# Attention scores in 32x64 tiles, with the keys summed down to 64 rows before the softmax sums

## The chip, the cores and the metric

The kernel runs on one core of a Trainium2 chip. A core has a matmul engine (TensorE, "PE" in the profile, with its weight loads as "PEld"), a vector engine (VectorE, "DVE"), an activation engine (ScalarE, "ACT"), a general engine (GpSimd, "POOL") and a queue engine (SyncE, "SP") that issues the transfers of this kernel. The metric is the device time of one execution in microseconds. All data is fp32.

## The reference

Two layers are applied to x of shape (8, 256, 64, 64). Layer 0 is an attention with 8 heads of 32 channels, in which the 4096 pixels of an image ask 256 keys that a 4x4 convolution with stride 4 makes. Layer 1 is a linear attention with depthwise convolutions, and takes no part in the change. Layer 0, cut to what matters:

```
xr  = conv(x, w_sr, stride 4); xr = layernorm over channels(xr)
q   = w_q x                            # 4096 tokens a batch
k,v = split(w_kv xr)                   # 256 keys a batch
for each of 8 heads (d = 32):
    sim  = q k^T / sqrt(32)            # 4096 x 256
    attn = softmax(sim over the keys)
    out  = attn v
x   = x + gamma * (w_out out)
```

## The kernel before

The kernel has three passes. The first makes layer 0 and the products w_qkv x of layer 1; the second and third do the rest of layer 1. The change is in the first pass, in the functions `keys_values`, `scores`, `valued`, `joined`, `counted`, `copied` and `normed`.

The first pass walks through 128 turns: 8 batches, 8 strips of 512 tokens (QB), 2 halves c of the channels (4 heads each). In a turn, the softmax is computed without a maximum, transposed: keys on partitions, tokens along the columns. `scores` (L820) is called twice a turn, for kc = 0 and 1, the two halves of 128 keys. For each head h it multiplies 32 rows of k (the head's channels, on partitions 32h to 32h+31, 128 keys as columns) with 32 rows of q and 512 tokens; the four heads stand on four different row groups of the array. ScalarE takes exp of each bank (L830) into a tile e of 128 keys by 512 tokens. `valued` (L843) multiplies v (128 keys by 32 channels of a head) with e (128 by 512) and adds the two kc in PSUM; the four heads stand in four column groups. The denominators come from `joined` (L857): GpSimd adds the e of kc = 0 and of kc = 1 for each head (L861); and from `counted` (L865): a matrix of ones (128 by 32) times this sum gives each token's sum over the keys, on 32 partitions. `copied` (L870) takes the product with v out of PSUM on ScalarE. `normed` (L875) turns the sums by 32x32 blocks on VectorE (L881), takes reciprocals of the sixteen columns that are needed, spreads them with a second transpose and multiplies.

The order within turn n is written out in the loop at L1072: first scores of kc = 0 of turn n, then the products with v and the sums of turn n-1, then scores of kc = 1 of turn n and its additions on GpSimd, then copy and normalization of turn n-1. After these come, as a filling for TensorE, products of w_qkv x (`qkv`, L931, seven products for a pair of parts, spread over the following turns), the queries of the next turn (L806), every second turn the output product `added` (L898) and, for turns 6 to 15 of a batch, the convolution and layernorm of the next batch's keys (`keys_values`, L725, a generator that is advanced step by step). A scheduler places instructions of an engine by these priorities; the first five turns of all have no qkv products to fill with. `differences` (L912) makes inputs of qkv, three on VectorE and one on GpSimd (L919), every fourth turn.

PSUM has eight banks, given out in rotation by `bank` (L641). Two are kept out of the rotation while they are in use: "av" from `valued` to `copied`, and "den" from `counted` to the first transpose in `normed`. `given_back` returns them to the end of the rotation.

Tiles on SBUF rotate by their number of buffers: e has 12 (E_BUFS), ej (the sum over kc) 4. `keys_values` uses one ring "ln" of 3 buffers for xr, sq and wide. v of a batch is kept in `vv`, 128 keys by 2 halves by 256 channels; kk and vv have two buffers each, so that the next batch's are made while the present batch's are read.

An fp32 matmul is two MATMUL rows and two LDWEIGHTS rows in the profile.

Of the kernel before, what the change touches and what calls it, by code (L numbers as in the profile page):

```python
# [27 lines left out]
F32 = mybir.dt.float32  # L28
AF = mybir.ActivationFunctionType
ALU = mybir.AluOpType  # L30
# [25 lines left out]
RS = 16  # L56
NS = HH // RS
BR = QB // WW
PE_TAPS = 6


# [563 lines left out]
def first_pass(ctx: ExitStack, tc: tile.TileContext, a, fine, planes, x2d, kd, vd, ready):  # L625
# [15 lines left out]
    def bank(name, keep=None):  # L641
        i = turns.pop(0)
        if keep:
            kept[keep] = i
        else:
            turns.append(i)
        return psum.tile([P, 512], F32, tag=f"bank{i}", name=name)
# [75 lines left out]
    kks, vvs = {}, {}  # L723

    def keys_values(b):  # L725
        ln = lambda name: keys.tile([P, 2, NK], F32, tag="ln", name=f"{name}_{b}", bufs=3)
        xr = ln("xr")

        ps = bank(f"sr_{b}", "sr").rearrange("p (o k) -> p o k", o=2)
        taps = sorted((phase(dy, dx), dy * R + dx) for dy in range(R) for dx in range(R))  # L730
        for f, tap in taps:
            w = keys.tile([P, 2, C], F32, tag="wsr", name=f"wsr_{b}_{f}", bufs=3)
            nc.sync.dma_start(w, a.w_sr[:, :, tap])
            for ci in range(2):
                for oc in range(2):
                    nc.tensor.matmul(  # L736
                        ps[:, oc],
                        w[:, ci, oc * P : (oc + 1) * P],
                        strips(b, f // 2)[:, ci, f % 2 * NK : (f % 2 + 1) * NK],
                        start=(f == ci == oc == 0),  # L740
                        stop=(f == R * R - 1 and ci == 1),
                        skip_group_check=True,
                    )
            yield
        nc.scalar.copy(xr, ps)
        given_back("sr")
        yield

        mean = bank(f"mean_{b}")[:, :NK]
        for ci in range(2):  # L750
            nc.tensor.matmul(mean, mean_w, xr[:, ci], start=(ci == 0), stop=(ci == 1))
        for ci in range(2):
            nc.vector.tensor_sub(xr[:, ci], xr[:, ci], mean)
        sq = ln("sq")
        nc.vector.tensor_mul(sq, xr, xr)
        yield

        var = bank(f"var_{b}")
        for kc in range(2):
            for ci in range(2):  # L760
                nc.tensor.matmul(
                    var[:, kc : kc + 1],
                    sq[:, ci, kc * P : (kc + 1) * P],
                    mean_w[:, 0:1],
                    start=(ci == 0),
                    stop=(ci == 1),
                )
        rstd = two.tile([P, 2, 2], F32, tag="rstd", name=f"rstd_{b}")
        nc.vector.tensor_scalar_add(rstd[:, 0], var[:, 0:2], LN_EPS)
        nc.gpsimd.tensor_tensor(rstd[:, 1], rstd[:, 0], mhalf, ALU.pow)  # L770
        wide = ln("wide")
        nc.scalar.copy(wide[:, :, :P], rstd[:, 1].unsqueeze(2).to_broadcast([P, 2, P]))
        yield
        rs = bank(f"rs_{b}")[:, :NK]
        for kc in range(2):
            nc.tensor.matmul(rs[:, kc * P : (kc + 1) * P], wide[:, kc, :P], ident, start=True, stop=True)
        for ci in range(2):
            nc.vector.tensor_mul(xr[:, ci], xr[:, ci], rs)
            nc.vector.tensor_scalar(
                xr[:, ci], xr[:, ci], consts["vec"][:, 0, ci : ci + 1], consts["vec"][:, 1, ci : ci + 1], ALU.mult, ALU.add  # L780
            )
        yield
        kk = two.tile([P, 2, NK], F32, tag="kk", name=f"kk_{b}")
        vv = two.tile([P, 2, C], F32, tag="vv", name=f"vv_{b}")
        kks[b], vvs[b] = kk, vv
        for oc in range(2):
            ps = bank(f"k_{b}_{oc}")[:, :NK]
            for ci in range(2):
                nc.tensor.matmul(
                    ps, consts["wkv"][:, ci, oc * P : (oc + 1) * P], xr[:, ci], start=(ci == 0), stop=(ci == 1)  # L790
                )
            nc.scalar.copy(kk[:, oc], ps)
        yield
        for kc in range(2):
            ps = bank(f"v_{b}_{kc}")[:, :C]
            for ci in range(2):
                nc.tensor.matmul(
                    ps, xr[:, ci, kc * P : (kc + 1) * P], consts["wkv"][:, ci, C:], start=(ci == 0), stop=(ci == 1)
                )
            nc.scalar.copy(vv[:, kc], ps)  # L800
        yield


# [15 lines left out]

    def scores(b, s, c, kc, qs):  # L820
        scs = [bank(f"sc_{b}_{s}_{c}_{kc}_{h}") for h in range(4)]
        for h in range(4):
            rows = slice(h * D0, (h + 1) * D0)
            nc.tensor.matmul(  # L824
                scs[h], kks[b][rows, c, kc * P : (kc + 1) * P], qs[rows], start=True, stop=True
            )
        es = []
        for h in range(4):
            e = two.tile([P, QB], F32, tag="e", name=f"e_{b}_{s}_{c}_{kc}_{h}", bufs=E_BUFS)
            nc.scalar.activation(e, scs[h], AF.Exp, scale=D0**-0.5)  # L830
            es.append(e)
        return es
# [9 lines left out]

    def valued(b, s, c, kc, es):  # L843
        if kc == 0:
            sums["av"] = bank(f"av_{b}_{s}_{c}", "av")
        for h in range(4):
            cols = slice(h * D0, (h + 1) * D0)
            nc.tensor.matmul(  # L848
                sums["av"][cols],
                vvs[b][:, kc, c * P + h * D0 : c * P + (h + 1) * D0],  # L850
                es[h],
                start=(kc == 0),
                stop=(kc == 1),
            )


    def joined(b, s, c, es0, es1):  # L857
        both = []
        for h in range(4):
            e = halves.tile([P, QB], F32, tag="ej", name=f"ej_{b}_{s}_{c}_{h}", bufs=4)  # L860
            nc.gpsimd.tensor_tensor(e, es0[h], es1[h], ALU.add)  # L861
            both.append(e)
        return both

    def counted(b, s, c, es):  # L865
        sums["den"] = bank(f"den_{b}_{s}_{c}", "den")
        for h in range(4):
            nc.tensor.matmul(sums["den"][h * D0 : (h + 1) * D0], ones_w, es[h], start=True, stop=True)  # L868

    def copied(b, s, c):  # L870
        att[b, s, c] = rest.tile([P, QB], F32, tag="att", name=f"att_{b}_{s}_{c}", bufs=4)
        nc.scalar.copy(att[b, s, c], sums["av"])
        given_back("av")

    def normed(b, s, c):  # L875
        den = sums["den"]
        i = 2 * ((b * NG + s) * 2 + c)
        turn = rest.tile([P, NB, D0], F32, tag="rden", name=f"rden_{b}_{s}_{c}", bufs=1)
        one = two.tile([P, NB], F32, tag="one", name=f"one_{b}_{s}_{c}")

        tc.keep_in_program_order(nc.vector.transpose(turn.rearrange("p n d -> p (n d)"), den))  # L881
        given_back("den")
        nc.vector.reciprocal(one, turn[:, :, 0])
        r = rest.tile([P, NB, D0], F32, tag="rall", name=f"rall_{b}_{s}_{c}", bufs=1)
        nc.vector.transpose(r, one.unsqueeze(2).to_broadcast([P, NB, D0]))
# [1136 lines left out]
```

## Time and profile before

| | before |
|---|---|
| median of 3 runs | 3618.5 us (3616.45 to 3620.99) |
| the profiled execution | 3620.12 us, span 3618.3 us |
| TensorE granted clock | 0.989 |
| PE busy | 3536.7 us (98%), 24738 rows |
| DVE busy | 2221.5 us (61%) |
| POOL busy | 1525.8 us (42%) |
| ACT busy | 1461.8 us (40%) |
| PE in scores, L824 | 292.9 us, 2048 rows |
| PE in products with v, L848 | 248.3 us, 2048 rows |
| PE in sums, L868 | 137.8 us, 1024 rows |
| POOL in additions, L861 | 679.0 us, 512 rows of 1354 ns |

A row of the groups gives line, engine, operation, output and inputs, shapes and count, then the busy time of the group, the mean length of one and the engine's idle time before them with what ended it. "32*128" after a matmul is the part of the array that it uses, rows by columns. Busy times are unions, so that four matmuls side by side count once. In the timeline a row has start, length, engine and line, and merges like instructions; "PE" rows end where a model puts the end, so that a group's cost is better read from the start of the next group.

### The profile page before, as it was taken

What the parts mean: (1) busy time and instruction counts of PE and PEld (TensorE: products, weight loads), DVE (VectorE), ACT (ScalarE), POOL (GpSimd) and SP (SyncE); (2) the same over time, 40 slices, a digit from 0 to 9 for tenths busy, and PEclk for the clock granted to TensorE, in tenths of its full rate; (3) what the DMA queues carried; (4) which work ended last, traced back from release to release, by engine and by line L of the source; (5) the groups of instructions that cost most, each with busy time, mean ns of one, the idle gap of its engine ahead of it and who ended that gap; (6) DMA issues with size and microseconds to landing.
All of it is one profiled execution on the core that took longest, in us unless ns stands there. A gap on an engine that the chain in (4) does not pass through costs nothing.

```text
span 3618.3 us, 64503 instructions
## 1 busy us (share of the span) xinstructions
PE 3536.7 (98%) x24738; PEld 1937.9 (54%) x24738; DVE 2221.5 (61%) x3371; ACT 1461.8 (40%) x3241; POOL 1525.8 (42%) x1506
## 2 busy tenths in 40 slices
PE   8999999999999999999999999999999999999998
PEld 4443534434435344344334788888888874333333
DVE  1557466565574665655777777777777774444442
ACT  2444344354443443544553444444444423333332
POOL 2434344343343443433443566566656541222222
PEclk9999999999999999999999999999999999999999
DMA  5345445455454454553645999999999977787773
GB/s 176 99 113 147 134 98 158 112 140 136 106 148 130 101 156 107 131 147 98 161 116 134 267 250 263 265 259 255 264 264 255 261 236 212 222 228 229 222 220 95
DMA packets 574780, 643.44 MB, mean 178 GB/s; under 512 B 81408, under 2 KB 450560, under 8 KB 574464
## 3 DMA queue, kind: packets, MB, share of 16 engines
q1 hardware_dynamic: 574464, 639.24, 64.0%
q8 instruction: 197, 3.23, 0.4%
q14 instruction: 119, 0.97, 0.1%
HBM read 389.85 MB, written 249.23 MB: 177 GB/s over the span
## 4 chain that ended last, share of the span: by engine, by line
PE 87%; DMA 6%; DVE 3%; ACT 1%; SPq 1%; issue 1%; POOL 0%; POOLq 0%; DVEq 0%; ACTq 0%
PE qkv L946 16%; PE p L1740 11%; PE cv L1313 8%; PE sc L824 8%; PE av L848 7%; PE o L902 6%; PE q L809 6%; PE sr L736 6%; PE cv L1344 6%; PE sums L1399 6%; PE den L868 3%; DMA raw<-planes 2%; DMA vq<-v 2%; PE rep L1726 2%; PE den L1707 1%
## 5 line engine op out<-in xcount | busy, mean ns | idle before, releaser
L861 POOL TENSOR_TENSOR ej<-e,e 128x512 f32<-128x512 f32 x512 | 679.0, 1354 | 950.5 <-ACT e L830 950.5
L830 ACT ACTIVATE e<-sc 128x512 f32<-128x512 f32 x1024 | 529.3, 608 | 568.6 <-PE sc L824 568.6
L1313 PE MATMUL cv<-w,c 128*128 128x128 f32 x3072 | 388.9, 280 | 12.8 <-DVE stage L959 6.7
L1313 PEld LDWEIGHTS cv<-w,c 128*128 128x128 f32 x3072 | 366.1, 195 | 14.6 <-issue 6.7
L1750 POOL TENSOR_TENSOR y<-z,xs 128x512 f32<-128x512 f32 x128 | 165.5, 1302 | 463.1 <-ACT z L1748 434.2
L824 PE MATMUL sc<-q,kk 32*128 32x512 f32 x2048 | 292.9, 639 | 0.0
L946 PE MATMUL qkv<-differences,combined 128*128 128x512 f32 x576 | 291.3, 597 | 0.4 <-POOL differences L919 0.3
L1399 PE MATMUL sums<-vq,r 128*32 128x288 f32 x4096 | 265.5, 408 | 0.0
L1740 PE MATMUL p<-raw,wp 128*128 128x512 f32 x512 | 248.8, 608 | 9.9 <-ACT z L1748 9.9
L848 PE MATMUL av<-e,vv 128*32 128x512 f32 x2048 | 248.3, 598 | 0.6 <-ACT e L830 0.6
L881 DVE STREAM_TRANSPOSE rden<-den 128x512 f32<-128x512 f32 x128 | 91.5, 715 | 254.6 <-PE den L868 252.4
L1330 ACT ACTIVATE r<-s 128x512 f32<-128x512 f32 x128 | 81.0, 632 | 411.8 <-DVE s L1329 402.6
L736 PE MATMUL sr<-x,wsr 128*128 128x256 f32 x1024 | 234.5, 383 | 9.4 <-DMA wsr<-in_w_sr_dram 9.3
L809 PE MATMUL q<-x,wq 128*128 128x512 f32 x512 | 241.9, 594 | 0.0
L1740 PE MATMUL p<-agg,wp 128*128 128x512 f32 x512 | 241.2, 593 | 0.0
L902 PE MATMUL o<-att,wout 128*128 128x512 f32 x512 | 230.4, 592 | 0.0
L736 PEld LDWEIGHTS sr<-x,wsr 128*128 128x128 f32 x1024 | 195.8, 192 | 63.2 <-issue 34.5
L817 ACT COPY q<-q 128x512 f32<-128x512 f32 x128 | 75.1, 586 | 373.4 <-PE q L809 373.4
L962 DVE TENSOR_TENSOR whole<-part,qkv 128x512 f32<-128x512 f32 x256 | 172.7, 684 | 73.4 <-ACT part L1008 54.0
L1344 PE MATMUL cv<-y,w 128*128 128x128 f32 x1536 | 204.0, 278 | 6.9 <-DVE y L1265 4.1
L1399 PEld LDWEIGHTS sums<-vq,r 128*32 128x32 f32 x4096 | 156.0, 110 | 75.2 <-issue 1.2
L946 PE MATMUL qkv<-x,wqkv 128*128 128x512 f32 x384 | 188.8, 611 | 5.2 <-ACT e L830 5.2
(162 smaller groups left out, 5734.8 us busy)
## 6 DMA issues: line engine op xcount, KB each, us to landing
planes<-stage SPq DMA_DIRECT2D x128, 578.0 KB
d<-planes SPq DMA_DIRECT2D x128, 578.0 KB
vq<-v SPq DMA_DIRECT2D x256, 256.0 KB
raw<-planes SPq DMA_DIRECT2D x64, 578.0 KB
x<-in_xp_dram SPq DMA_DIRECT2D x64, 512.0 KB
wsr<-in_w_sr_dram SPq DMA_DIRECT2D x128, 256.0 KB
x<-x SPq DMA_DIRECT2D x128, 256.0 KB
k<-turned SPq DMA_DIRECT2D x256, 128.0 KB
```

Of the source, the lines that this page charges most:

```text
L736: nc.tensor.matmul(ps[:, oc], w[:, ci, oc * P : (oc + 1) * P], strips(b, f // 2)[:, ci, f % 2 * NK : (f % 2 + 1) * NK], start=(f == ci == ...
L809: nc.tensor.matmul(ps, consts["wq"][:, ci, c * P : (c + 1) * P], strips(b, s)[:, ci], start=(ci == 0), stop=(ci == 1),)
L824: nc.tensor.matmul(scs[h], kks[b][rows, c, kc * P : (kc + 1) * P], qs[rows], start=True, stop=True)
L830: nc.scalar.activation(e, scs[h], AF.Exp, scale=D0**-0.5)
L848: nc.tensor.matmul(sums["av"][cols], vvs[b][:, kc, c * P + h * D0 : c * P + (h + 1) * D0], es[h], start=(kc == 0), stop=(kc == 1),)
L861: nc.gpsimd.tensor_tensor(e, es0[h], es1[h], ALU.add)
L902: nc.tensor.matmul(ps, consts["wout"][:, c, oc * P : (oc + 1) * P], att[c], start=(c == 0), stop=(c == 1))
L946: nc.tensor.matmul(ps, w, x, start=True, stop=True)
L1313: nc.tensor.matmul(ps[:, g * P : (g + 1) * P], c[:, g, cols], w[:, g, n * P : (n + 1) * P], start=(da == 0), stop=(da == 1),)
L1344: nc.tensor.matmul(out, w[:, g], x, start=True, stop=True)
L1399: nc.tensor.matmul(ps[h * D0 : (h + 1) * D0, : 36 * D1].rearrange("p (r n e) -> p r n e", r=3, e=D1), kt[:, par, h, 2 * r + c], vq[:, r : ...
L1740: nc.tensor.matmul(as_block(ps, i // 2), wp[:, i, oc * P : (oc + 1) * P], block(g, i // 2, i % 2, j), start=(i == 0), stop=(i == 3),)
```

## The change

In the score products, each head's matmul of 32 rows by 128 keys, 512 tokens, is replaced by four: for each quarter kq of 64 keys and each half of the tokens one of 32 rows by 64 keys and 256 tokens. The two halves of the tokens go to the two halves of the partitions of the output (rows 0 to 63 and 64 to 127), and the two quarters of keys of a kc to its two halves of columns. So a tile e has the same size as before, but its rows 0 to 63 hold 64 keys for the first 256 tokens, rows 64 to 127 the same 64 keys for the last 256 tokens, and its column halves two quarters of keys.

The products with v are done in 64 rows (keys) by 32 columns (channels), 256 tokens: one for each quarter, head and half of the tokens, four quarters added in PSUM. The two halves of the tokens go to two banks, av0 and av1, 256 columns of each. v is needed on both halves of the partitions for every quarter, so `vv` grows to four quarters, ScalarE copies each v product in two halves, and two transfers per batch copy each half to the other partitions.

`joined` adds the e of both kc as before (ej, now with one buffer), then adds the two column halves (ef, 128 by 256): this sums the keys down to 64 rows for each half of the tokens. `counted` multiplies ones of 64 rows by 32 columns with 256 columns of ef, for each head and half, into the other 256 columns of av0 and av1. There is no bank "den" any more; av0 and av1 are given back after the transposes in `normed`, and `copied` and the first transpose are done in two parts of 256 columns. Ring "ln" shrinks to two buffers and wide gets a tile of its own.

```diff
--- before.py
+++ after.py
@@ -56,6 +56,8 @@
 RS = 16
 NS = HH // RS
 BR = QB // WW
+HALVES = slice(0, P // 2), slice(P // 2, P)
+QH = slice(0, QB // 2), slice(QB // 2, QB)
 PE_TAPS = 6
 
 
@@ -723,7 +725,7 @@
     kks, vvs = {}, {}
 
     def keys_values(b):
-        ln = lambda name: keys.tile([P, 2, NK], F32, tag="ln", name=f"{name}_{b}", bufs=3)
+        ln = lambda name: keys.tile([P, 2, NK], F32, tag="ln", name=f"{name}_{b}", bufs=2)
         xr = ln("xr")
 
         ps = bank(f"sr_{b}", "sr").rearrange("p (o k) -> p o k", o=2)
@@ -768,12 +770,12 @@
         rstd = two.tile([P, 2, 2], F32, tag="rstd", name=f"rstd_{b}")
         nc.vector.tensor_scalar_add(rstd[:, 0], var[:, 0:2], LN_EPS)
         nc.gpsimd.tensor_tensor(rstd[:, 1], rstd[:, 0], mhalf, ALU.pow)
-        wide = ln("wide")
-        nc.scalar.copy(wide[:, :, :P], rstd[:, 1].unsqueeze(2).to_broadcast([P, 2, P]))
+        wide = keys.tile([P, 2, P], F32, tag="wide", name=f"wide_{b}", bufs=1)
+        nc.scalar.copy(wide, rstd[:, 1].unsqueeze(2).to_broadcast([P, 2, P]))
         yield
         rs = bank(f"rs_{b}")[:, :NK]
         for kc in range(2):
-            nc.tensor.matmul(rs[:, kc * P : (kc + 1) * P], wide[:, kc, :P], ident, start=True, stop=True)
+            nc.tensor.matmul(rs[:, kc * P : (kc + 1) * P], wide[:, kc], ident, start=True, stop=True)
         for ci in range(2):
             nc.vector.tensor_mul(xr[:, ci], xr[:, ci], rs)
             nc.vector.tensor_scalar(
@@ -781,7 +783,7 @@
             )
         yield
         kk = two.tile([P, 2, NK], F32, tag="kk", name=f"kk_{b}")
-        vv = two.tile([P, 2, C], F32, tag="vv", name=f"vv_{b}")
+        vv = two.tile([P, 4, C], F32, tag="vv", name=f"vv_{b}")
         kks[b], vvs[b] = kk, vv
         for oc in range(2):
             ps = bank(f"k_{b}_{oc}")[:, :NK]
@@ -797,7 +799,10 @@
                 nc.tensor.matmul(
                     ps, xr[:, ci, kc * P : (kc + 1) * P], consts["wkv"][:, ci, C:], start=(ci == 0), stop=(ci == 1)
                 )
-            nc.scalar.copy(vv[:, kc], ps)
+            for h, rows in enumerate(HALVES):
+                nc.scalar.copy(vv[rows, 2 * kc + h], ps[rows])
+        for h, rows in enumerate(HALVES):
+            nc.sync.dma_start(vv[HALVES[1 - h], h::2], vv[rows, h::2])
         yield
 
 
@@ -819,11 +824,17 @@
 
     def scores(b, s, c, kc, qs):
         scs = [bank(f"sc_{b}_{s}_{c}_{kc}_{h}") for h in range(4)]
-        for h in range(4):
-            rows = slice(h * D0, (h + 1) * D0)
-            nc.tensor.matmul(
-                scs[h], kks[b][rows, c, kc * P : (kc + 1) * P], qs[rows], start=True, stop=True
-            )
+        for kq in range(2 * kc, 2 * kc + 2):
+            for h in range(4):
+                rows = slice(h * D0, (h + 1) * D0)
+                for half in range(2):
+                    nc.tensor.matmul(
+                        scs[h][HALVES[half], QH[kq % 2]],
+                        kks[b][rows, c, kq * P // 2 : (kq + 1) * P // 2],
+                        qs[rows, QH[half]],
+                        start=True,
+                        stop=True,
+                    )
         es = []
         for h in range(4):
             e = two.tile([P, QB], F32, tag="e", name=f"e_{b}_{s}_{c}_{kc}_{h}", bufs=E_BUFS)
@@ -842,44 +853,51 @@
 
     def valued(b, s, c, kc, es):
         if kc == 0:
-            sums["av"] = bank(f"av_{b}_{s}_{c}", "av")
-        for h in range(4):
-            cols = slice(h * D0, (h + 1) * D0)
-            nc.tensor.matmul(
-                sums["av"][cols],
-                vvs[b][:, kc, c * P + h * D0 : c * P + (h + 1) * D0],
-                es[h],
-                start=(kc == 0),
-                stop=(kc == 1),
-            )
+            sums["av"] = [bank(f"av_{b}_{s}_{c}_{half}", f"av{half}") for half in range(2)]
+        for kq in range(2 * kc, 2 * kc + 2):
+            for h in range(4):
+                cols = slice(h * D0, (h + 1) * D0)
+                for half, rows in enumerate(HALVES):
+                    nc.tensor.matmul(
+                        sums["av"][half][cols, : QB // 2],
+                        vvs[b][rows, kq, c * P + h * D0 : c * P + (h + 1) * D0],
+                        es[h][rows, QH[kq % 2]],
+                        start=(kq == 0),
+                        stop=(kq == 3),
+                    )
 
 
     def joined(b, s, c, es0, es1):
         both = []
         for h in range(4):
-            e = halves.tile([P, QB], F32, tag="ej", name=f"ej_{b}_{s}_{c}_{h}", bufs=4)
+            e = halves.tile([P, QB], F32, tag="ej", name=f"ej_{b}_{s}_{c}_{h}", bufs=1)
             nc.gpsimd.tensor_tensor(e, es0[h], es1[h], ALU.add)
-            both.append(e)
+            f = halves.tile([P, QB // 2], F32, tag="ef", name=f"ef_{b}_{s}_{c}_{h}", bufs=4)
+            nc.gpsimd.tensor_tensor(f, e[:, QH[0]], e[:, QH[1]], ALU.add)
+            both.append(f)
         return both
 
     def counted(b, s, c, es):
-        sums["den"] = bank(f"den_{b}_{s}_{c}", "den")
         for h in range(4):
-            nc.tensor.matmul(sums["den"][h * D0 : (h + 1) * D0], ones_w, es[h], start=True, stop=True)
+            for half, rows in enumerate(HALVES):
+                nc.tensor.matmul(
+                    sums["av"][half][h * D0 : (h + 1) * D0, QH[1]], ones_w[rows], es[h][rows], start=True, stop=True
+                )
 
     def copied(b, s, c):
         att[b, s, c] = rest.tile([P, QB], F32, tag="att", name=f"att_{b}_{s}_{c}", bufs=4)
-        nc.scalar.copy(att[b, s, c], sums["av"])
-        given_back("av")
+        for half in range(2):
+            nc.scalar.copy(att[b, s, c][:, QH[half]], sums["av"][half][:, : QB // 2])
 
     def normed(b, s, c):
-        den = sums["den"]
         i = 2 * ((b * NG + s) * 2 + c)
         turn = rest.tile([P, NB, D0], F32, tag="rden", name=f"rden_{b}_{s}_{c}", bufs=1)
         one = two.tile([P, NB], F32, tag="one", name=f"one_{b}_{s}_{c}")
 
-        tc.keep_in_program_order(nc.vector.transpose(turn.rearrange("p n d -> p (n d)"), den))
-        given_back("den")
+        flat = turn.rearrange("p n d -> p (n d)")
+        for half in range(2):
+            tc.keep_in_program_order(nc.vector.transpose(flat[:, QH[half]], sums["av"][half][:, QH[1]]))
+            given_back(f"av{half}")
         nc.vector.reciprocal(one, turn[:, :, 0])
         r = rest.tile([P, NB, D0], F32, tag="rall", name=f"rall_{b}_{s}_{c}", bufs=1)
         nc.vector.transpose(r, one.unsqueeze(2).to_broadcast([P, NB, D0]))
```

## The prediction

> **What bounds the kernel now.** I read the page's slices and its chain first: who is busy, and whose work ends last.
>
> ```profile
> PE   8999999999999999999999999999999999999998
> PE 87%; DMA 6%; DVE 3%; ACT 1%; SPq 1%; issue 1%; POOL 0%; POOLq 0%; DVEq 0%; ACTq 0%
> ```
>
> TensorE is busy in nearly every slice and carries 87% of the chain. The change lies in the first pass, about 60 to 1945 us. There I took two whole turns (one turn: 512 tokens, one half of the channels) from the windows view; its columns are length, PE, PEld, DVE, ACT, POOL.
>
> ```profile
> 803.82:816.60 12.78, 12.78 (x63) 4.64 (x59) 8.48 (x13) 6.17 (x15) 5.41 (x4) 1.00 0.85 290
> 816.60:829.38 12.78, 12.78 (x63) 4.64 (x59) 9.63 (x15) 5.58 (x14) 5.54 (x5) 1.00 0.73 145
> ```
>
> TensorE fills all 12.78 us; the others leave 3 us or more. So a microsecond off TensorE's row is a microsecond off the turn, until another engine's chain becomes as long. The timeline of TensorE prices the three groups touched; differences of starts are used, since the ends are modelled.
>
> ```profile
> 802.75 1.14 PE L824 MATMUL sc<-q,kk 32*128 32x512 f32 x8
> 803.82 1.92 PE L848 MATMUL av<-e,vv 128*32 128x512 f32 x16
> 805.56 1.04 PE L868 MATMUL den<-ej,ones_w 128*32 128x512 f32 x8
> 806.53 1.14 PE L824 MATMUL sc<-q,kk 32*128 32x512 f32 x8
> 807.61 1.12 PE L946 MATMUL qkv<-differences,wqkv 128*128 128x512 f32 x2
> ```
>
> Each fp32 matmul is two rows. Scores take 1.07 us, the v products 1.74, the sums 0.97. The weight loads show how they run:
>
> ```profile
> 804.28 0.13 PEld L848 LDWEIGHTS av<-e,vv 128*32 128x32 f32 x4 [0.30 <-issue]
> 804.71 0.13 PEld L848 LDWEIGHTS av<-e,vv 128*32 128x32 f32 x4 [0.30 <-issue]
> ```
>
> Four tiles start together, then 0.43 us pass: a wave of four side by side, 512 columns long. Last, who feeds the sums:
>
> ```profile
> 807.75 2.06 ACT L830 ACTIVATE e<-sc 128x512 f32<-128x512 f32 x4 [0.91 <-PE sc L824]
> 808.43 5.41 POOL L861 TENSOR_TENSOR ej<-e,e 128x512 f32<-128x512 f32 x4 [5.05 <-ACT e L830]
> ```
>
> GpSimd adds from 808.43 to 813.84; the sums that use this start at 818.34. The slack is 4.5 us. These are the rows for prices:
>
> ```profile
> L861 POOL TENSOR_TENSOR ej<-e,e 128x512 f32<-128x512 f32 x512 | 679.0, 1354 | 950.5 <-ACT e L830 950.5
> L868 PE MATMUL den<-ej,ones_w 128*32 128x512 f32 x1024 | 137.8, 592 | 0.4 <-POOL ej L861 0.4
> L1294 POOL TENSOR_TENSOR red_agg<-red_agg 128x256 f32<-128x256 f32 x64 | 57.7, 901 | 5.0
> L1294 POOL TENSOR_TENSOR red_raw<-red_raw 128x256 f32<-128x256 f32 x64 | 53.6, 837 | 2.7
> L1382 PE MATMUL raw<-vq,kq 128*32 128x32 f32 x4096 | 49.3, 199 | 0.0
> ```
>
> **What the Trainium skill says.** "TensorEngine Tiling (Array Packing)", sections Available Configurations and Key Properties: 32×64 and 64×32 both give eight tiles that work independently, and a change of mode drains the array. The trace agrees as far as it goes: four row tiles (scores) and four column tiles (v products) run side by side, and about 0.1 us is lost at each mode change. Eight tiles of rows and columns at once are in no row. "TensorE: Matmul & The Clock Gate", section Measured speedup vs the span model, gives 10.6 times for sixteen 32-by-32 tiles, so rows and columns combine; the trace can't confirm it. The Tiling page's Instruction Overhead gives about 60 cycles for each matmul. The trace is cheaper: 4096 rows of L1382 in 49.3 us, 12 ns each. Eight rows a wave are 0.1 us, below the 0.215 us that a wave of 256 columns lasts. "GPSIMD Engine Reference", Specifications: GpSimd's SBUF interface is shared with VectorE, and suffers from VectorE operations with two SBUF inputs. The trace agrees: most ej take 1.26 us, those beside the multiplication L887 up to 1.72.
>
> **The change, part by part.** TensorE first, for one turn.
>
> Scores (twice): 4 matmuls become 16, each half as wide and half as long. Waves go from 2 of 0.43 to 4 of 0.215: 0.86 us both. Of the 0.21 us beside the waves, about 0.107 is the first weight load of 128 columns (single rows: the first wave lasts 534 ns, the next 427), and about 0.09 the drain. 64 columns halve the load: -0.05. Eight tiles started 6.7 ns apart (single rows) instead of four add 0.03. Group: 1.05, gain 0.02, twice 0.04.
>
> Products with v: 8 matmuls become 32; 4 waves of 0.43 become 8 of 0.215, unchanged. The sums: 4 matmuls of 128 rows by 512 become 8 of 64 rows by 256, 2 waves of 0.43 become 2 of 0.215: -0.43. The later start of eight tiles costs 0.03, once. Sum: -0.04 - 0.43 + 0.03 = -0.44; I take -0.43.
>
> GpSimd: 4 operations of 128x256 more, with L1294 as the nearest row: same width, also dependent on the operation just before. Undisturbed it takes 0.73 us (median of red_raw), disturbed up to 1.1; its wait leaves a gap of 0.08 in the single rows. Since ej has one buffer now, each ej also waits for the ef before it: 0.08 again. So 1.26 + 0.08 + 0.73 + 0.08 = 2.15 for a head, 8.5 for four, and 0.45 for the meeting with L887: 8.96 instead of 5.4. The extra 3.55 us fit into the slack of 4.5 with 0.95 to spare. In the order of the sums it is a loop: scores start, 1.90 until the first addition (806.53 to 808.43), 8.96, 0.55 for the last head's sum and the drain, next scores: 11.4 us. TensorE's turn becomes 12.35 or more, so it stays the longer. Lower bound of the ef: 0.66 (half of an ej); upper: 1.06, every one disturbed.
>
> At the start the loop does decide. The first five turns have no qkv products and take 7.3 to 11.4 us; that part of the trace runs from 60.97 (first ej) to 104.30 (sixth turn's second scores). After: 60.97 + 8.6 + 0.5 = 70.1, then four loops of 11.4: 115.7. Loss: 11 us, gain included. The last turn, 9.99 us now, pays 1.5 the same way.
>
> TensorE's order is the same otherwise, except that in seven turns a product with v or some sums stand apart from their group: 14 more mode changes at 0.15 (drain and load), 2 us.
>
> ScalarE: att in two copies of 0.37 (row L800) for one of 0.60, +0.14, and once a batch four vv copies for two, +0.75: under its 6 us of idle in a turn. These copies now wait for the sums too, which share the bank: about 806.1, and ScalarE isn't free for them before 806.24. VectorE: the transpose L881 (0.715) in two, about +0.15 from the 0.41 of a 128x256 row (L778); 3 us idle cover it. Both banks come back after these transposes, as den's did; six other banks are used first. Without that cover a late bank would stop scores by those tenths.
>
> SP: two more DMAs of 128 KB a batch, behind a wait for the vv copies. Behind them on SP stand two weight loads at the start and stores later; nobody waits for these within microseconds. At the start v must land before 61.5, the copies end near 57.8: I count 0, at most 3 us once. Later batches have v made turns ahead. Fewer ln buffers and a smaller wide: same operations, 0.
>
> Sum: 123 turns × -0.43 = -53; +11 +1.5 +2. The net is -38 against the profiled execution's 3620.1 (span 3618.3): 3582. The median of the runs is 1.6 lower: 3580.
>
> **The rivals.** (A) GpSimd takes over: if the ef meet VectorE's two-input work (differences L917 to L920, L887) as the disturbed half of L1294 did, 1.06 us each, the chain is 10.3, the loop 12.7 to 12.8 in the 56 shortest turns, more where memsets or L919 fall in. For: margin of 0.95 us only. Against: VectorE's work beside additions in the trace mostly reads PSUM, and those ej took 1.26. It decides from about 0.25 us of ef beyond 0.73; at 1.06 replaying the additions after the profile's ready times gives no gain to 20 us loss, with memsets in the chain 60: 3620 to 3680. This is the case on the other side.
>
> (B) The eight tiles don't run side by side. Should row tiles exclude each other in 64×32, the ten waves double: +2.15 - 0.43 = 1.7 a turn, 220 us, 3840; in scores alone +1.3 a turn, 3785; both 4060. For: no row shows it. Against: both forms run singly, and issue at 12 ns suffices.
>
> (C) The gain is there but small: waves of 256 columns carry a fixed cost of 20 ns more, 18 waves are 0.36 us a turn. 3605 to 3625, no change.
>
> **How the numbers follow.** Main case 0.61 (3565 to 3603), A 0.13, B 0.11, C 0.10 (about half beyond -0.2%), still faster 0.05 (no loss at the start, loads wholly hidden: 3555). A measurement tells 0.2%, 7 us, from no change. Faster: 0.61 + 0.05 + 0.05 = 0.71; same: 0.05 of C and 0.03 of A, 0.08; slower: 0.10 of A and B, 0.21. The range leaves out B and the ends of A and of the fast case: 3556 to 3645. The likeliest case alone has 3565 to 3603.
>
> **What would show it.** The sums' group from 0.97 to about 0.5 us between starts, v products still 1.74, scores 1.05; 38000 PE rows instead of 24738; turns of 12.35 for 12.78; ef near 0.75, its chain near 9 us, and no wait of the sums for it after the fifth turn; about 11 us lost by 116 us. The prediction fails if the v products' group grows (B), or if TensorE idles before the sums in the steady turns (A).

## The result and the profile after

The changed kernel takes 3681.3 us (median of 4 runs, 3667.9 to 3683.2); the kernel before, beside it on the same chip, 3617.5 (3616.2 to 3621.0). The ratio is 1.0167, with an interval of 1.0142 to 1.0192: 1.7% slower, where 1% faster was predicted. The profiled execution is the one of 3681.4 us; its span is 3679.6 us, 61.3 more than before.

First the page of the changed kernel: TensorE's slices, and the groups of the two additions.

```profile
PE   7999999999999999999999899999999999999998
L874 POOL TENSOR_TENSOR ej<-e,e 128x512 f32<-128x512 f32 x512 | 660.3, 1290 | 423.1 <-ACT e L841 394.8
L876 POOL TENSOR_TENSOR ef<-ej 128x256 f32<-128x256 f32 x512 | 410.7, 802 | 38.3
```

The slices look as they did; the loss is spread too thin for tenths. The second addition takes 0.80 us on the mean, near the 0.73 that was assumed. The page's chain can't be used here: it reaches back only to 2018 us, past the first pass. Now the timeline of TensorE in a steady turn; differences of starts are read.

```profile
799.93 1.12 PE L831 MATMUL sc<-q,kk 32*64 32x256 f32 x32
800.97 1.96 PE L861 MATMUL av<-e,vv 64*32 64x256 f32 x64
802.73 0.64 PE L883 MATMUL av<-ef,ones_w 64*32 64x256 f32 x16
803.29 1.12 PE L831 MATMUL sc<-q,kk 32*64 32x256 f32 x32
804.34 1.13 PE L964 MATMUL qkv<-differences,wqkv 128*128 128x512 f32 x2
```

Scores 1.04 to 1.05 us (before 1.07), products with v 1.76 (1.74), sums 0.56 (0.97). On TensorE the change does what was predicted. Two turns in the windows view (length, PE, PEld, DVE, ACT, POOL, then clock, share of the transfers and GB/s): turn 35, which lost, and a steady one:

```profile
588.93:603.69 14.76, 13.24 (x164) 6.21 (x163) 8.29 (x13) 6.35 (x16) 11.74 (x15) 1.00 0.52 161
803.29:815.63 12.34, 12.34 (x170) 6.00 (x162) 10.03 (x14) 5.70 (x17) 9.86 (x9) 1.00 0.84 185
```

The steady turn is 12.34 us for 12.78, the predicted gain of 0.44. But not all turns are steady. A turn is measured here from its first score matmul to that of the next, and n is its number. The 127 differences between the kernels sum to +71.4 us, in six kinds of turn:

| turns | count | before to after, us | at -0.44 each it would be |
|---|---|---|---|
| n = 0 to 5, the start | 6 | +14.1 | (predicted +11) |
| n%4 == 3 | 30 | +50.8 | -13.2 |
| n%16 == 9 | 8 | +17.3 | -3.5 |
| n%16 == 12 | 8 | +5.5 | -3.5 |
| n%4 == 2 | 31 | +3.0 | -13.6 |
| the others | 44 | -19.2 | -19.4 |

The kind that lost most, n%4 == 3, has this in GpSimd's timeline around turns 34 and 35 (turn 34 starts at 575.06):

```profile
576.11 0.74 POOL L876 TENSOR_TENSOR ef<-ej 128x256 f32<-128x256 f32 x1
585.25 0.16 POOL L943 MEMSET stage<- 128x68 f32 x1 [8.41 <-DMA planes<-stage]
585.47 0.22 POOL L944 MEMSET stage<- 128x68 f32 x1
585.58 1.26 POOL L874 TENSOR_TENSOR ej<-e,e 128x512 f32<-128x512 f32 x1
```

A "stage" is a tile in which `qkv` collects planes with a border of zeros before they are stored; `new_stage` sets the border on GpSimd (L943, L944). There is one buffer for each of two kinds, so its memset waits until the transfer that stores the older stage has read it. Here this memset stands ahead of the additions of turn 34, and the queue works in order. In the kernel before, the first addition of turn 34 starts 6.7 us after the turn's first scores, and 6.8 us after in the changed kernel with the memsets out of the way (below); here it starts 10.5 us after: 3.7 us late. The sums that need it stand in the next turn on TensorE:

```profile
591.73 0.92 PE L883 MATMUL av<-ef,ones_w 64*32 64x256 f32 x12
594.16 0.62 PE L883 MATMUL av<-ef,ones_w 64*32 64x256 f32 x4 [1.52 <-POOL ef L876]
594.72 1.12 PE L831 MATMUL sc<-q,kk 32*64 32x256 f32 x32
```

Their last head waits, and everything behind on TensorE waits with it. In the kernel before, the same memset was queued behind the additions of that turn, with the next addition 5 us later (at 565.83), and cost nothing:

```profile
553.11 4.96 POOL L861 TENSOR_TENSOR ej<-e,e 128x512 f32<-128x512 f32 x4 [7.74 <-ACT e L830]
560.28 0.16 POOL L925 MEMSET stage<- 128x68 f32 x1 [1.84 <-DMA planes<-stage]
```

### The profile page after: what moved, and what is told of

Read it like the earlier page. It is cut to its first block, busy times and chain, and to the rows that moved or that the text cites. A ratio compares the mean times of both kernels' runs of the same rounds, so it can differ in the third digit from the quotient of the medians.

```text
span 3679.6 us, 92633 instructions
## 1 busy us (share of the span) xinstructions
PE 3530.2 (96%) x38050; PEld 2120.4 (58%) x38050; DVE 2202.6 (60%) x3499; ACT 1484.5 (40%) x3385; POOL 1909.7 (52%) x2018
## 5 line engine op out<-in xcount | busy, mean ns | idle before, releaser
L874 POOL TENSOR_TENSOR ej<-e,e 128x512 f32<-128x512 f32 x512 | 660.3, 1290 | 423.1 <-ACT e L841 394.8
L876 POOL TENSOR_TENSOR ef<-ej 128x256 f32<-128x256 f32 x512 | 410.7, 802 | 38.3
L899 DVE STREAM_TRANSPOSE rden<-av 128x256 f32<-128x256 f32 x256 | 99.8, 428 | 412.6 <-ACT att L890 412.5
L831 PE MATMUL sc<-q,kk 32*64 32x256 f32 x8192 | 296.2, 395 | 0.0
L738 PE MATMUL sr<-x,wsr 128*128 128x256 f32 x1024 | 238.8, 388 | 20.3 <-DMA wsr<-in_w_sr_dram 20.3
L861 PE MATMUL av<-e,vv 64*32 64x256 f32 x8192 | 255.4, 382 | 0.5 <-ACT e L841 0.5
L831 PEld LDWEIGHTS sc<-q,kk 32*64 32x64 f32 x8192 | 155.4, 133 | 150.6 <-issue 104.4
L861 PEld LDWEIGHTS av<-e,vv 64*32 64x32 f32 x8192 | 148.1, 107 | 98.3 <-issue 39.5
```

Of the source, the lines that this page charges most:

```text
L738: nc.tensor.matmul(ps[:, oc], w[:, ci, oc * P : (oc + 1) * P], strips(b, f // 2)[:, ci, f % 2 * NK : (f % 2 + 1) * NK], start=(f == ci == ...
L831: nc.tensor.matmul(scs[h][HALVES[half], QH[kq % 2]], kks[b][rows, c, kq * P // 2 : (kq + 1) * P // 2], qs[rows, QH[half]], start=True, sto ...
L861: nc.tensor.matmul(sums["av"][half][cols, : QB // 2], vvs[b][rows, kq, c * P + h * D0 : c * P + (h + 1) * D0], es[h][rows, QH[kq % 2]], st ...
L876: nc.gpsimd.tensor_tensor(f, e[:, QH[0]], e[:, QH[1]], ALU.add)
```

## The experiments

All ratios are to the kernel before in the same session. "First pass" is the sum over the 127 turns, in the profiled execution, against before (after: +71.4).

**The tiles without the second addition.** In `joined` and `counted`, with ej in four buffers and whole in five (the diff is cut; `...` stands for what was left out):

```diff
-            f = halves.tile([P, QB // 2], F32, tag="ef", ...)
-            nc.gpsimd.tensor_tensor(f, e[:, QH[0]], e[:, QH[1]], ALU.add)
+        for k in range(2):
+            for h in range(4):
+                for half, rows in enumerate(HALVES):
+                    nc.tensor.matmul(sums["av"][half][h * D0 : (h + 1) * D0, QH[1]], ones_w[rows],
+                        es[h][rows, QH[k]], start=(k == 0), stop=(k == 1))
```

> The new tiles for scores, products with v and sums, without the second addition on GpSimd: the sums add both column halves of ej on TensorE (16 matmuls of 64 rows by 256 columns a turn in place of 8), ej has four buffers again and whole five. Theory (the loss comes from the additions on GpSimd and from what stands around them in its queue): TensorE has four waves of 0.215 us for the sums as before, so the turns stay at 12.7 to 12.8 us and the start loses nothing: 3612 to 3622 us. Rival (the small tiles or the shared bank of products and sums cost the time): 3650 us or more.

Measured: 3639.7 us, ratio 1.0060 (1.0042 to 1.0079); first pass +26.2, of which +21.5 lies in the turns n%16 == 9 and +3.1 in n%4 == 2. Neither side was right: the start and the turns n%4 == 3 lost nothing (+0.1 each), but something else did. TensorE's timeline of this kernel in turn 25:

```profile
418.32 1.92 PE L861 MATMUL av<-e,vv 64*32 64x256 f32 x52
421.83 3.72 PE L738 MATMUL sr<-x,wsr 128*128 128x256 f32 x16 [1.59 <-DMA wsr<-in_w_sr_dram]
425.48 0.43 PE L861 MATMUL av<-e,vv 64*32 64x256 f32 x6
```

Eight matmuls of the next batch's reduction (sr, two rows each) stand in the middle of the products with v, and wait for their weights. In this kernel they were put there without any wait for GpSimd. So this split is not the second addition's doing. Nor is the place of the memset: here too it stands ahead of the additions, as in turn 34, which starts at 553.70:

```profile
564.93 0.16 POOL L946 MEMSET stage<- 128x68 f32 x1 [12.93 <-DMA planes<-stage]
565.25 4.97 POOL L874 TENSOR_TENSOR ej<-e,e 128x512 f32<-128x512 f32 x4
```

The four additions start 11.5 us after the first scores, and the turns n%4 == 3 lose nothing. So the scheduler's new order came with the tiles; the longer chain made it dear. The split was taken out by itself: the two steps of sr at the end of the turns n%16 == 8 go to the next turn.

```diff
-        for _ in range(taps):                           # the second two steps of a turn
+        for _ in range(taps * (at != 8)):
-        for _ in range(taps):                           # the first two
+        for _ in range(taps * (2 if at == 9 else 1)):
```

> As e1_tiles_only (new tiles, no second addition on GpSimd), with the two sr steps of the turns n%16==8 left to the next turn as in e3, so that the sums stand together. Theory (the tiles themselves cost nothing; the whole loss of e1 was the sums split by sr matmuls in seven turns, 22 us): 3618 us, the same as before (3611 to 3624). Rival (the tiles or the shared bank cost something of their own in every turn): 3630 us or more.

Measured: 3619.8 us, ratio 1.0001 (0.9990 to 1.0011); the turns n%16 == 9 at 0.0, the first pass at +5.6. The theory holds: 32x64 and 64x32 tiles, the shared bank and the doubled v cost nothing that the times show. The gain of 0.44 us, and the losses at the start and in the turns n%4 == 3 and n%16 == 12, appear only with the second addition. The turns n%4 == 2 stand at +3.2 here as well; they come back below.

**The memsets behind the additions.** The changed kernel with

```diff
-        nc.gpsimd.memset(st[:, :, 0 if g // 2 else NB], 0.0)
+        tc.keep_in_program_order(nc.gpsimd.memset(st[:, :, 0 if g // 2 else NB], 0.0))
```

and the same for the second memset. `keep_in_program_order` holds an instruction behind the one that its engine was given last.

> The changed kernel with one thing moved: the memsets of a stage stand in GpSimd's queue behind the additions of the turn in which they are made, not ahead of them; all other engines keep their order. Theory (a memset that waits for the transfer of the older stage holds up the additions behind it): the turns n%4==3 fall from about 15.1 to 12.3 us, 23 times 2.8, so 3617 us (3608 to 3632). Rival (eight additions a turn are too long for GpSimd wherever the memsets stand): 3665 us or more.

Measured: 3632.3 us, ratio 1.0036 (1.0023 to 1.0049); first pass +21.9. The turns n%4 == 3 went from +50.8 to +3.1. The waits of TensorE for the second addition in the first pass, of the changed kernel and then of this one (total us, times, longest):

```profile
PE av L883 <- POOL ef L876: 29.9, 26, 1.8
```

```profile
PE av L883 <- POOL ef L876: 4.7, 3, 1.8
```

The three waits that are left belong to the start (turns 4 and 5); from turn 6 to 126 there is none. Nothing but the place of memsets in one queue was changed, and 48 of the 64 us that these turns had missed came back (49 over all turns). The chain of eight additions fits, with 0.35 to 1 us between its end and the sums in the steady turns; the rival that it doesn't is out. The time is at the upper edge of what was expected, since 16 us of the 64 did not come back. They lie in the turns n%16 == 11 alone, and have another cause (the power of rstd, below). The first addition of turn 34 now starts 6.84 us after the turn's first scores:

```profile
572.48 1.27 POOL L874 TENSOR_TENSOR ej<-e,e 128x512 f32<-128x512 f32 x1 [4.28 <-ACT e L841]
573.83 1.06 POOL L876 TENSOR_TENSOR ef<-ej 128x256 f32<-128x256 f32 x1
```

**Is a delayed chain dear by itself?** The kernel before, with the waiting pair of memsets made a turn earlier and the additions held behind it:

```diff
+            ahead_of = [f.made for f in todo.get(n + 1, []) if n % 4 == 2 and hasattr(f, "made")]
+            for f in ahead_of:
+                f()                                     # makes the stages of turn n+1
-            ej[n] = joined(*order[n], *es[n])
+            ej[n] = joined(*order[n], *es[n], bool(ahead_of))   # True: additions in program order
```

> The kernel before, with one pair of memsets of a stage placed ahead of the four additions of the turns n%4==2, as the scheduler placed it in the changed kernel; all other engines keep their order. Theory (the additions start 3.7 us late by it, and the kernel before has 4.5 us of room where the changed one has 0.95): the same time as before, ratio 0.998 to 1.003. Rival (the delay costs by itself, whatever the room): 60 us more, ratio 1.015 or more.

Measured: 3620.0 us, ratio 1.0003 (0.9991 to 1.0015); first pass +0.1. GpSimd and TensorE of this kernel, turn 34 starting at 545.52:

```profile
556.05 4.95 POOL L861 TENSOR_TENSOR ej<-e,e 128x512 f32<-128x512 f32 x4
```

```profile
562.12 1.04 PE L870 MATMUL den<-ej,ones_w 128*32 128x512 f32 x8
563.09 1.14 PE L824 MATMUL sc<-q,kk 32*128 32x512 f32 x8
```

The additions start 10.5 us after the first scores, as late as in the changed kernel, and end at 561.0, before the sums at 562.12. So the same order of the queue costs nothing with four additions. With eight it costs 0.6 to 2.6 us a time on the mean, by the kind of turn (the changed kernel against the run with the memsets behind): the slack is what the change used up.

**The sums kept together.** The memsets behind, and the sr steps of the turns n%16 == 8 left to the turn after, as above.

> As e2_memsets_behind, and in the turns n%16==8 two steps of the next batch's reduction (sr) are left to the turn after, so that the sums of a turn stand together on TensorE. Theory: the seven turns n%16==9 lose 2.5 us by the split (two more changes of mode, and sums behind a weight transfer), so 16 to 20 us less than e2: about 3599 us (3590 to 3606). Rival (the sr matmuls only fill a time in which the sums would wait for ef): same as e2 within 5 us.

Measured: 3616.3 us, ratio 0.9988 (0.9978 to 0.9998); first pass +4.6. The turns n%16 == 9 went from +18.5 to -3.5, which is -0.44 each; 4 us came up again in n%16 == 12. The theory holds for the difference, 16 us between the two runs; the 3599 us had counted from a better run with the memsets behind.

**The start, first try.** For n < 5, heads 2 and 3 on VectorE:

```diff
+            if h > 1 and b == 0 and 2 * s + c < 5:
+                nc.vector.tensor_tensor(f, es0[h][:, QH[0]], es0[h][:, QH[1]], ALU.add)
+                for half in QH:
+                    nc.vector.tensor_tensor(f, f, es1[h][:, half], ALU.add)
+                continue
```

> As e3_sums_together, and in the first five turns of the kernel heads 2 and 3 are added on VectorE (three operations of 128x256 each), GpSimd keeps heads 0 and 1. Theory (the start loses 14 us because each turn there waits for all eight additions on GpSimd): the loop becomes 1.9 + 4.3 + 0.55 = 6.8 us, below what these turns took before, so 10 to 15 us less than e3: about 3586 us. Rival (VectorE's two-input additions slow GpSimd's so far that little is gained): 0 to 5 us less.

Measured: 3617.7 us, ratio 0.9992 (0.9979 to 1.0005); start +15.4 where it had been +13.9. Theory and rival both lost. Turns 1 and 2 were indeed shorter (12.7 and 9.7 us for 16.3 and 15.3), but turns 3 and 5 grew (15.6 and 20.3 us for 7.6 and 14.7): the time went over to TensorE's waits for VectorE, where the additions stand ahead of the transposes that give the banks back and of the normalization:

```profile
72.83 1.55 PE L861 MATMUL av<-e,vv 64*32 64x256 f32 x43 [1.64 <-DVE rden L904]
82.15 0.64 PE L831 MATMUL sc<-q,kk 32*64 32x256 f32 x2 [1.68 <-DVE rden L904]
84.24 3.65 PE L925 MATMUL o<-att,wout 128*128 128x512 f32 x4 [1.45 <-DVE att L910]
```

**The power of rstd.** In `keys_values`, GpSimd's power is queued behind the eight additions now, and ScalarE waits for it with the copy that widens it, with the copy of q behind. ScalarE's timeline in the run with the sums kept together, turn 75:

```profile
1201.38 0.40 ACT L774 COPY wide<-rstd 128x256 f32<-128x256 f32 x1 [8.21 <-POOL rstd L772]
1201.69 0.58 ACT L822 COPY q<-q 128x512 f32<-128x512 f32 x1
```

The matmuls of the queries end at 1196.4, so their copy goes 5 us late, and the next scores need it. The product `rs`, which needs the widened copy, stands ahead of these scores on TensorE and waits too (first pass of the changed kernel, total us, times, longest):

```profile
PE rs L778 <- ACT wide L774: 13.8, 7, 2.0
```

The kernel before has no such wait of TensorE after the start. On top of the run with the sums kept together (not of the try above), the copy and what follows it were traced a turn later:

```diff
+        yield
+        yield
         wide = keys.tile([P, 2, P], F32, tag="wide", name=f"wide_{b}", bufs=1)
```

> As e3_sums_together, and the widening of rstd on ScalarE, with what follows it in the making of keys and values, comes one turn later, so that neither ScalarE nor TensorE stands waiting for the power on GpSimd, which is queued behind the eight additions. Theory: the seven turns n%16==11 and 12 give back the 1.3 us and 2.5 us that they lose against the others, 15 to 22 us in all: about 3597 us. Rival (those waits only move to the next turn): within 5 us of e3.

Measured: 3619.7 us, ratio 1.0000 (0.9984 to 1.0016); first pass +9.5. A miss: the two yields move the work in program order, but the scheduler put the copy back ahead of the copy of q, and in place of `rs` the scores waited for q (17.2 us in 7 waits).

**The start, second try.** For n < 5 no second addition; ej goes to four buffers of the tag whole, which no one uses yet, and TensorE sums both column halves as in the first experiment.

```diff
+            if b == 0 and 2 * s + c < 5:
+                e = halves.tile([P, QB], F32, tag="whole", name=f"ej_{b}_{s}_{c}_{h}", bufs=6)
+                nc.gpsimd.tensor_tensor(e, es0[h], es1[h], ALU.add)
+                both.append(e)
+                continue
...
+        parts = 2 if b == 0 and 2 * s + c < 5 else 1
```

> As e5_rstd_early, and in the first five turns the sums take both halves of ej on TensorE (16 matmuls a turn), without the second addition, with ej in four buffers of the tag whole, idle then. Theory (the 14 us of the start are the wait for the second additions): 11 to 14 us less than e5, about 3584 us. Rival (the start loses by the shared bank of products and sums, which is given back later, as e4 hints): 5 us or less.

Measured: 3608.0 us, ratio 0.9969 (0.9957 to 0.9982), 11.7 us below the run before it; start +0.1 for +13.4. Theory and size of the difference hold: those turns wait for the additions, and the loop through GpSimd sets their length.

**The stage copies.** Left are, among others, the turns n%4 == 2. There ScalarE makes four copies into a stage (2.2 us) ahead of the copies of att and the exponentials, and a product of TensorE (qkv) waits for the last of these: 30 times in the first pass of the changed kernel, 18.4 us in all, against 7 times and 5.2 us in the kernel before. They were put behind the exponentials:

```diff
-                    tc.keep_in_program_order(nc.scalar.copy(inside, rows(whole)))
+                    later.append(lambda: tc.keep_in_program_order(nc.scalar.copy(inside, rows(whole))))
...
         for f in products[:3]:
             f()
+        for f in later:
+            f()
+        later.clear()
```

and the stores of the stages likewise.

> As e6_start_whole, and the four stage copies on ScalarE (2.2 us in one turn of four) stand behind the exponentials of the turn, not ahead of the copies of att. Theory (in the turns n%4==2 the two copies of att and the exponentials end too late for the qkv products, 0.5 us a turn): 31 times 0.5, 10 to 16 us less than e6, about 3570 us. Rival (the wait goes over to the transposes or to the stores of the stages): no gain.

Measured: 3580.6 us, ratio 0.9896 (0.9868 to 0.9923), 27 us below the run before it. The gain was there, and twice what was expected; the kernel before was then given the same edit alone:

> The kernel before, with the stage copies on ScalarE moved as in e7, and nothing else. Theory (in the kernel before these turns waited 0.15 us, the rest of the gain of e7 belongs to the changed kernel): 3 to 6 us less than before, ratio 0.998 to 1.000. Rival (the stage copies cost the kernel before as much as the changed one): 13 us or more less, ratio below 0.9965.

Measured: 3600.8 us, ratio 0.9945 (0.9924 to 0.9967): 17 us less, the rival's side by the median of four runs. But in its first pass the turns n%4 == 2 give only 10.6 us, 7 us of that in n%16 == 10, which is between theory and rival; its span is 21.3 us shorter, so some 11 us lie outside the turns. What gives them stays open, and executions of one kernel differ by as much (the kernel before: 3610.4 to 3629.2 in that session). In the turns, then, 10.6 of the 27 us belong to an edit that helps either kernel, and 17 to a wait that the change had made: the turns n%4 == 2 of the two kernels with this edit differ by the 0.44 us each that was due. By the medians it is 17 and 10; the time of the runs does not settle it closer.

**The widening held back.** To the run of the stage copies:

```diff
-        nc.scalar.copy(wide, rstd[:, 1].unsqueeze(2).to_broadcast([P, 2, P]))
+        tc.keep_in_program_order(nc.scalar.copy(wide, rstd[:, 1].unsqueeze(2).to_broadcast([P, 2, P])))
```

> As e7_stage_copies_later, with the copy that widens rstd held in ScalarE's queue behind the copies of att of the next turn, so that the copy of q is not queued behind a wait for GpSimd's power. Theory (e5 gained nothing because the scheduler put that copy back ahead of the copy of q, and the scores waited for q in place of rs): the turns n%16==11 fall by 2.1 us and n%16==12 by about 1 us, seven times each, so 15 to 22 us less than e7: about 3561 us. Rival (the time of these turns is that of their own matmuls): within 5 us of e7.

Measured: 3550.1 us, ratio 0.9793 (0.9776 to 0.9809), 30 us below the run before it, more than expected; the first pass went from -31.2 to -57.2, 18 us of it in the turns n%16 == 11 and 8 in n%16 == 12. In the run of the stage copies TensorE's waits in the first pass still had

```profile
PE sc L833 <- ACT q L824: 17.6, 7, 2.7
```

and in this one, up to the last turn, TensorE has only this wait for another engine:

```profile
PE sc L833 <- DVE xr L782: 1.7, 7, 0.3
```

This version is 2.1% faster than the kernel before, and 1.4% faster than the kernel before with the stage copies moved (3550.1 against 3600.8 us): 51 us, about the 53 that 0.43 us in 123 turns had come to; in the sum over the turns it is 46.6 (57.2 less 10.6). The other edits were not run on the kernel before. From 100 us to the end of its first pass TensorE has one kind of wait for another engine there, the one that the stage copies make, so its trace shows nothing that the others could remove:

```profile
PE qkv L946 <- ACT e L830: 5.2, 7, 0.7
```

The sums over the kinds of turn, in us against before, show each edit in its place. From the column "start whole" on, the key and value matmuls of a batch stand one turn later, so n%16 == 12 is counted together with the others. What the last edit gives in the row n%4 == 3 lies in the turns n%16 == 11.

| turns | after | memsets behind | sums together | start whole | stage copies | widening held |
|---|---|---|---|---|---|---|
| start, 6 | +14.1 | +13.5 | +13.9 | +0.1 | +0.1 | +0.1 |
| n%4 == 3, 30 | +50.8 | +3.1 | +3.3 | +1.5 | +1.9 | -16.2 |
| n%16 == 9, 8 | +17.3 | +18.5 | -3.5 | -3.5 | -3.5 | -3.5 |
| n%4 == 2, 31 | +3.0 | +3.1 | +3.0 | +3.5 | -24.1 | -24.2 |
| n%16 == 12 and others, 52 | -13.7 | -16.2 | -12.0 | -5.4 | -5.4 | -13.4 |
| sum | +71.4 | +21.9 | +4.6 | -3.8 | -31.2 | -57.2 |

## Why the prediction was wrong

**The work on TensorE: right.** The three groups came out at 1.05, 1.76 and 0.56 us against 1.05, 1.74 + 0.03 and 0.54, the steady turn at 12.34 for 12.35. What the prediction took from the Trainium skill, "TensorEngine Tiling (Array Packing)", sections Available Configurations and Key Properties, that 32x64 and 64x32 give eight tiles that work independently, no row showed then; the rows of this trace do: eight start within 0.05 us, and the next eight follow 0.22 to 0.26 us after them. Rival B is out, and so is C: e1b has the same waves of 256 columns and the time of before.

**The step that failed** is "The extra 3.55 us fit into the slack of 4.5 with 0.95 to spare", in the use that was made of it. The sum was right, and not only for the turn that it was read in: the trace before has 4.5 us or more between the last addition and the sums in every turn from 6 to 126, and with the memsets out of the way TensorE never waits for the chain of 8.5 to 9 us in those turns. What failed is that the room was spent as if the changed kernel kept the order of GpSimd's queue. In every fourth turn a memset that waits for a transfer had moved ahead of the chain: 3.7 us of delay against about 1 us of room. The prediction had the words "with memsets in the chain 60: 3620 to 3680" as an afterthought to rival A, whose stated cause was another (second additions slowed by VectorE to 1.06 us, where the trace has 0.80 on the mean). That the measured time lies near the end of that range is luck. Of the 110 us between the predicted and the measured sum over the turns, the turns n%4 == 3 are 64. The memsets' place is shown to be 48 of these, and 49 of the total of the turns, by the run that changes nothing else; the other 16 are in the turns n%16 == 11 and belong to rstd.

**"TensorE's order is the same otherwise, except that in seven turns a product with v or some sums stand apart from their group: 14 more mode changes at 0.15, 2 us."** Seen and mis-sized: it measured 21 us (+17.3 where -3.5 was due). The split was priced by its changes of mode, and the matmuls put in between were taken to be free because they have to be done anyway. They aren't, since they wait for weights that would have landed by their old place: 1.10 us in the changed kernel, 1.59 in the run with tiles alone, with a part of the group left to be done behind them. That the turns n%16 == 9 get it all back where the split is removed is shown; how the 2.75 us of a turn divide between the wait, the changes of mode and the broken waves was not measured.

**ScalarE: "under its 6 us of idle in a turn".** An average over turns. In the turns n%4 == 2 the stage copies take 2.2 us just ahead of the two copies of att, and the gain of 0.44 was lost to a wait there, 16 us in all. It came back when these copies were moved. **The start**: predicted +11, measured +14.1, by the mechanism given; TensorE waits 11.7 us there for the second additions. **The power of rstd** behind the longer chain on GpSimd was in no step; of the making of keys the prediction has only "Fewer ln buffers and a smaller wide: same operations, 0". It cost 16 us in the turns n%16 == 11 and 9 in n%16 == 12, the second largest miss; in the last run holding the widening back gave 26. The copies of v, the two more transfers on SP and the smaller rings cost nothing, as said.

The terms together, as misses against the predicted -0.43 a turn: 48 (memsets) + 25 (rstd) + 19 (the split sums) + 16 (stage copies) + 3 (start) = 111, and -39 + 111 = +72, against +71.4 measured. The two later passes, which the change doesn't touch, gave some 10 us of it back in the profiled execution; why was not tried, and the kernel before differs by as much from one execution to another.

## What to carry to other kernels

Slack that is read in the kernel before holds for its order of the queues: before it is spent on a longer chain, look in each kind of turn of the changed kernel at what stands ahead of the chain in its engine's queue, above all at an instruction that waits for a transfer. Where a scheduler fills the queues, a change on one engine can move instructions on the others: here the memsets had moved with the new tiles alone, before any chain was longer. A new order can cost nothing until the slack behind it is used up; compare the orders of all engines, price each moved instruction by the wait that it carries and not by its own length, and pin those few. Here pinning or moving four kinds of instruction, and other sums in the first five turns, turned 1.7% slower into 2.1% faster, of which 0.3% (by the turns) to 0.5% (by the medians) would have been had without the change.

## What was not expected of the hardware

- Eight fp32 tiles of 32x64 or 64x32 cost the same as four of twice the size: the run with the tiles alone is at 1.0001 of before, with 40098 TensorE rows for 24738.
- A dependent addition on GpSimd starts 0.08 us after the one before it ends. The first ef of a chain takes 1.06 us and the others 0.73 in steady turns: about one in four is slowed, where about half of the red_agg rows that gave the price were.
- A memset of 0.16 us at the head of GpSimd's queue waited 8.4 us for a transfer, and held up additions that could have run for the last 3.7 of them. The profile books this as idle time of the memset's line, whose waits went from 43.8 us (24 times) to 241.3 us (30 times) in the first pass, while those of the additions fell from 924.3 to 370.0 us.
